# A conv block in five passes: the joins on either side of the second pass, rewritten

## The chip, the cores and the metric

The kernel runs on one core of one Trainium2 chip. The metric is the time of one execution on the device in microseconds (us). Three executions of the kernel before gave 5501.92, 5508.98 and 5525.27; the median, 5508.98, is its time. One further execution was profiled.

## The reference

x has 8 images of 96 x 96 pixels with 192 channels, all in float32. Two residual layers follow each other. What matters here is the first:

```
g      = groupnorm(x)                                  # 32 groups
proj   = g @ W_in + b_in                               # 192 -> 384 channels
local  = depthwise conv 3x3 (proj), zero padding
lr, rl = s[t] = 0.6 s[t-1] + 0.4 local[t], left to right and right to left
tb, bt = the same, downwards and upwards
mixed  = 0.25 (lr + rl + tb + bt) + local
x1     = x + (layernorm(mixed) * ln_g + ln_b) @ W_out + b_out
```

The second layer is: groupnorm of x1, depthwise 7x7 convolution, layernorm over channels, 192 -> 768 -> 192 with a gelu between, scaled and added to x1.

## The kernel before

The program is five passes, with everything between them in DRAM.

**Pass A** (lines 251 to 572) normalises, transposes and projects. It goes over 96 steps: eight images b, four blocks k of eight columns, and three parts j. Each three steps fill one buffer `po` (128 partitions; three blocks m of 128 channels; eight columns), which `store_a` (L425) writes to the DRAM tiles `P_d[g][m]` from the GpSimd (POOL) queue: three large stores `whole` (L430, 1152 KB each) and, where the columns lie at the edge of a 32-column block, small ones `edges` (L442). For the very last `po` the store of m = 0 is split over the POOL and ScalarE (ACT) queues, and the rest is handed on as `late_a`.

**Pass B** (602 to 788) does the convolution and the four scans. It takes 4 channels at a time, k = 0 to 95, in three thirds i: 288 steps n. One step: 24 matmuls on TensorE with a banded matrix (`conv_b`, L662; a float32 matmul shows as two records), copies out of PSUM by ACT (L671, L674), a scan along rows on VectorE (DVE) in one direction (L695) and, one step later, in the other (L704), a small scaling on POOL (L699); the column scans are a matmul (`mix_b`, L683 and L686, copied by ACT in L687), and POOL adds both (L746, three steps after the convolution). The inputs are `pin_k` (partitions 0 to 33 for images 0 to 3, 64 to 97 for images 4 to 7) and `band_k`, loaded from the SyncE (SP) queue by `load_pin_b` (L644, one large and two small DMAs for each half g) and `load_band_b` (L631). They are loaded three k ahead (`load_b(k + 3)`, L758). Each pair of k leaves one buffer `mo`, stored to DRAM by eight DMAs (`store_steps`, L706, issued at L718), two in each step, from the POOL queue; those of the last pair alternate between SP and POOL. `M_d` is two tiles: channels 0 to 255 and channels 256 to 383. Channels are done in order, so the first tile is complete after two thirds of the pass. The last k adds its first third on POOL and the others on DVE (L745).

The start of B, before: L731 to L739 load `pin` for k = 0, 1 with g = 0, then g = 1 and the bands, then everything for k = 2, and then run `late_a`. Images 4 to 7 (g = 1) need the last columns of the last image, so those loads wait for the last stores of A.

**Pass C** (1006 to 1200) turns the image: a unit u is one column of four images, 384 rows by 384 channels, 192 units. `load_c` (L1054) loads `mt` from both parts of M (L1060, 384 KB and 192 KB) and `xr` (L1067). For each of three blocks j, `block_c` (L1073) transposes three channel blocks (L1078), multiplies by the weights `wc` (L1080, three channel blocks accumulated in PSUM), and ACT takes mean and squares (L1082, L1084). POOL adds the constant `cst` to `xr` (L1170), DVE finishes one unit later (L1097). The weights are made at L1018 to L1045: `wc` = W_out scaled by ln_g less its column mean, `cst` = b_out + ln_b W_out; they come from the buffer `pre`, loaded six k before the end of B (L595).

**Passes D and E** (from L852) are the 7x7 convolution and the two dense layers. The change doesn't touch them.

What sets the order: the loops of A to E stand inside `tc.manual_schedule()`, so each engine and queue gets their instructions in the order in which the code calls them. The few statements between the loops (L611 to L613, L1017 to L1045, the three `load_c` at L1139) stand outside, and the planner places them: in the profile L1020 to L1024 run at 756 us, L1018 and the first L1033 at 1789 us. [...] On-chip memory of a finished pass is reused by the next, tile by tile, once the readers of the old tile are done.

## Time and profile before

| | us |
|---|---|
| median of the three timed executions | 5508.98 |
| profiled execution, its own time | 5497.31 |
| its span in the profile | 5495.5 |
| last matmul of A begins | 752.60, runs 2.21 |
| first matmul of B | 772.29 |
| first scan of B on DVE | 778.19 |
| last scans of B on DVE | 1793.25, run 3.37 |
| first transpose of C | 1818.35 |
| third unit of C, its first "mean" on ACT | 1829.23 |
| last matmuls of C, first of D | about 2629 |

In the profiled execution the span is 1.8 us shorter than the device time. A window view lists, for a stretch of the span, the busy time of each engine with the number of instructions, the granted clock of TensorE as a share of full speed (PEclk), the share of time in which the 16 DMA engines were busy, and the GB/s that they moved. A timeline lists instructions in order of their start: start, length, engine, line, operation, tiles, count, and in square brackets how long the engine had been idle and what released it. SPq, ACTq and POOL with DMA_DIRECT2D are the issue of a transfer, not the transfer.

### The profile page before, as it was taken

How to read it: one execution, taken by the hardware profiler on the slowest of the kernel's cores; microseconds unless marked ns; L12 is line 12 of the kernel's file. 1: busy time of each engine (PE TensorE's matmuls, PEld its weight loads, DVE VectorE, ACT ScalarE, POOL GpSimd, SP SyncE). 2: the span in 40 equal slices, each digit the busy share in tenths (PEclk: the TensorE clock that was granted, in tenths of full speed). 3: DMA queues.
4: the chain of work that ended last, by engine and by line, in shares of the span. 5: the costliest groups of instructions: out<-in, count | busy, mean ns of one | idle time of the engine just before them, and what ended most of it. 6: DMA issues, size and time to landing. Idle time of an engine off the chain costs nothing. (4 is left out here: it accounts for less than half of the span.)

```text
span 5495.5 us, 108054 instructions
## 1 busy us (share of the span) xinstructions
PE 5277.4 (96%) x42206; PEld 3357.6 (61%) x42206; DVE 3449.8 (63%) x6722; ACT 2586.1 (47%) x5778; POOL 2367.0 (43%) x2060
## 2 busy tenths in 40 slices
PE   6999989999999899999787899999999999999999
PEld 4666643333333799899444566666666676766767
DVE  6556549999999455555555545555566666656654
ACT  2444447777777466565434444444433333333332
POOL 1211128888888555555322232222233333333332
PEclk9999989999999999999888999999999999999999
DMA  7999869999998799899997454555433232333231
GB/s 219 286 289 276 244 188 245 244 244 243 245 243 218 233 291 294 263 287 308 287 302 176 120 137 121 131 138 136 114 89 80 79 79 79 88 90 86 79 79 41
DMA packets 793246, 1015.28 MB, mean 185 GB/s; under 512 B 331151, under 2 KB 668768, under 8 KB 790688
## 3 DMA queue, kind: packets, MB, share of 16 engines
q1 hardware_dynamic: 676488, 633.41, 44.1%
q0 software_dynamic: 84848, 334.59, 18.5%
q10 hardware_dynamic: 31400, 40.37, 3.3%
q8 instruction: 333, 5.46, 0.4%
q14 instruction: 177, 1.45, 0.1%
HBM read 603.70 MB, written 419.95 MB: 186 GB/s over the span
## 5 line engine op out<-in xcount | busy, mean ns | idle before, releaser
L1481 PEld LDWEIGHTS hp<-w1g,g 128*128 128x128 f32 x6912 | 1117.9, 190 | 140.7 <-issue 83.4
L1481 PE MATMUL hp<-w1g,g 128*128 128x192 f32 x6912 | 1174.9, 329 | 0.0
L1470 ACT ACTIVATE g<-hp,b0g 128x512 f32<-128x512 f32 x864 | 519.8, 692 | 1209.4 <-PE hp L1461 1186.1
L1500 POOL DMA_DIRECT2D out_dram<-xo x288 | 211.3, 734 | 1569.5 <-DVE xo L1492 1488.0
L1492 DVE TENSOR_TENSOR xo<-hp,r 128x384 f32<-128x384 f32 x288 | 229.1, 795 | 983.5 <-PE hp L1481 979.2
L1451 PE MATMUL hp<-yT,w0w 128*128 128x512 f32 x1728 | 779.3, 597 | 19.6 <-DVE yT L1436 19.6
L1080 PE MATMUL po<-wc,mt 128*128 128x193 f32 x3456 | 685.5, 334 | 9.8 <-DVE x1c L1097 9.2
L662 PE MATMUL pl<-pin,band 34*32 34x380 f32 (+1 forms) x13824 | 629.4, 490 | 17.5 <-issue 17.5
L746 POOL TENSOR_TENSOR mo<-mo,z 128x768 f32<-128x768 f32 x286 | 598.9, 2094 | 4.5 <-ACT mo L687 0.4
L1080 PEld LDWEIGHTS po<-wc,mt 128*128 128x128 f32 x3456 | 554.9, 191 | 41.3 <-ACT mean L1082 30.8
L1451 PEld LDWEIGHTS hp<-yT,w0w 128*128 128x128 f32 x1728 | 321.3, 190 | 379.7 <-issue 346.0
L695 DVE TENSOR_TENSOR_SCAN z<-decay,loc 128x768 f32<-128x768 f32 x288 | 505.9, 1757 | 38.7 <-ACT loc L671 9.6
L1244 PE MATMUL hp<-xin,band 63*64 63x372 f32 (+1 forms) x4608 | 420.7, 501 | 95.7 <-ACT yo L1254 35.2
L704 DVE TENSOR_TENSOR_SCAN z<-decay,z 128x768 f32<-128x768 f32 x288 | 498.4, 1731 | 0.1
L662 PEld LDWEIGHTS pl<-pin,band 34*32 34x32 f32 x13824 | 236.1, 107 | 392.8 <-issue 385.9
L1415 POOL TENSOR_TENSOR rs<-tot,neg_half 32x32 f32<-32x32 f32 x72 | 394.7, 5481 | 120.3 <-DVE tot L1413 92.5
L683 PE MATMUL pa<-loc,mix 128*32 128x384 f32 x3456 | 431.9, 493 | 0.0
L686 PE MATMUL pa<-last,down 96*32 96x384 f32 x1152 | 426.8, 493 | 0.9 <-ACT mo L687 0.9
L1461 PE MATMUL hp<-yT,w0w 64*128 64x512 f32 x1728 | 419.5, 611 | 0.0
L1254 ACT ACTIVATE yo<-hp,dwb 128x384 f32<-128x384 f32 x384 | 197.0, 584 | 435.6 <-PE hp L1244 285.0
L671 ACT COPY loc<-pl 128x384 f32<-128x384 f32 x576 | 248.0, 483 | 310.7 <-PE pl L662 310.7
L395 PE MATMUL pm<-xT,win 128*128 128x384 f32 x1152 | 392.4, 491 | 0.0
(155 smaller groups left out, 7237.6 us busy)
## 6 DMA issues: line engine op xcount, KB each, us to landing
pin<-P SPq DMA_DIRECT2D x192, 576.0 KB
P<-po POOLq DMA_DIRECT2D x95, 1152.0 KB, 9.9
mt<-M SPq DMA_DIRECT2D x192, 384.0 KB
xq<-in_x_dram SPq DMA_DIRECT2D x96, 576.0 KB
xr<-in_x_dram SPq DMA_DIRECT2D x192, 288.0 KB
X<-x1c SPq DMA_DIRECT2D x144, 384.0 KB
out_dram<-xo POOLq DMA_DIRECT2D x288, 192.0 KB, 2.5
r<-X SPq DMA_DIRECT2D x35, 1536.0 KB
```

The lines of the kernel that those rows point to most:

```text
L662: nc.tensor.matmul(pls[g][at * RB : (at + 1) * RB, :, lo:hi], band[rows, c, kh, :], pin[rows, c, :, NJ - 1 - j, lo + kh - 1 : hi + kh - 1] ...
L683: nc.tensor.matmul(pa[at], mix[:, i, at], loc[:, q], start=True, stop=True)
L686: nc.tensor.matmul(pa[at], down[:, to], last[:, q], start=True, stop=True)
L695: nc.vector.tensor_tensor_scan(zf, decay_f, loc.rearrange("p q n -> p (q n)"), 0.0, ALU.mult, ALU.add)
L704: nc.vector.tensor_tensor_scan(zr, decay_f, zr, 0.0, ALU.mult, ALU.add)
L746: eng.tensor_tensor(m, m, z, ALU.add)
L1080: nc.tensor.matmul(po, lhs[m], wc[:, m], start=(m == 0), stop=(m == NC - 1))
L1244: nc.tensor.matmul(pys[g][k * 64 : (k + 1) * 64, :, lo:hi], band[rows, k * GS + c, d * ZS : d * ZS + 64], xin[rows, :, :, k * GS + c, lo + ...
L1451: nc.tensor.matmul(hps[m, q], w0w[:, 0, m * 128 : (m + 1) * 128], yT[:, 2 * q], start=True, stop=False,)
L1461: nc.tensor.matmul(hps[m, q], w0w[p, 1, m * 128 : (m + 1) * 128], yT[p, 1], start=False, stop=True,)
L1470: nc.scalar.activation(g[:, m, q], hps[m, q], AF.Gelu, bias=b0g[:, m : m + 1], scale=1.0)
L1481: nc.tensor.matmul(po[:, q], g[:, m, q, k * 128 : (k + 1) * 128], w1g[:, m], start=(m == 0), stop=(m == NE - 1),)
```

## The change

At the join of A and B:

- A DRAM tile `PL_d` holds the last eight columns of the last image for channels 0 to 7 only (73,728 bytes). One DMA on SP writes it from `po`; `last_pin_b` reads it back into `pin_0` (SP) and `pin_1` (ACT), two DMAs each.
- The other parts of `pin_0` and `pin_1` are cut such that they don't touch what the last `po` holds: for g = 1 five DMAs in place of three. They, and the bands, stand ahead of the `PL_d` store on SP.
- The last large stores (`late_a`) are all on POOL now and stand behind steps 1 and 2 of B; `whole(0)` and `edges(0)` are first. The loads of k = 2 follow: half g = 0 in step 0, half g = 1 and the band in step 1, with all of k = 3 behind them.

At the join of B and C:

- The stores of the last `mo` but one go to SP. Those of the last are held back (`late_b`) and issued on ACT in `make_wc`, behind three ACT instructions that scale `wc`.
- All three adds of the last k are on DVE.
- `mean_w` and `lnb` are made on POOL six and four k before the end of B, `wc` is scaled on ACT, `blk` and `pick` are filled on POOL; the matmuls and subtractions of L1036 to L1045 stay, in another order.
- Units 0 to 2 have their `mt` in a tile of the pool `early` (a place that the buffer `yo` of pass D takes later). Their channels 0 to 255 are loaded ahead of the last stores; then, before the rest has come, unit 0 is transposed for those channels and blocks j = 0 and 2 of units 0 and 1 are multiplied for them.
- `block_c` is split into `turn_c`, `project_c` and `square_c`; a third of the channels is left to do for what was begun.
- The two x1c buffers become two pools of one buffer.

And everything from pass A on is put inside one `manual_schedule()`: all in written order.

```diff
+    CC, WA = 4, 8
+    PL_d = dram.tile([WA, 2 * CC, NJ, S], F32, name="PL_d")
...
+            steps = [lambda m=m: whole(m, nc.gpsimd) for m in range(NC)]
+            steps += [lambda m=m: edges(m, nc.gpsimd) for m in range(NC)]
             if final:
-                whole(0, nc.gpsimd, slice(0, 64))
-                edges(0, nc.scalar)
-                whole(0, nc.scalar, slice(64, 128))
-                steps = [lambda m=m: whole(m, nc.gpsimd) for m in range(1, NC)]
-                return steps + [lambda m=m: edges(m, nc.gpsimd) for m in range(1, NC)]
-            for m in range(NC):
-                whole(m, nc.gpsimd)
-            for m in range(NC):
-                edges(m, nc.gpsimd)
+                return steps[::NC] + [f for n, f in enumerate(steps) if n % NC]
+            for step in steps:
+                step()
...
+        ctx.enter_context(tc.manual_schedule())
...
     def load_pre():
+        nc.gpsimd.memset(mean_w, 1.0 / C)
...
+    def spread_pre():
+        for m in range(NC):
+            nc.gpsimd.tensor_copy(lnb[:, m], gb[:, 1, m : m + 1].to_broadcast([128, 128]))
...
+        def load_pin_b(k, g, last=False):
...
+            def part(lo, hi, b=slice(0, GB), j=slice(0, NJ)):
                 nc.sync.dma_start(
-                    pin[p + lo : p + hi].rearrange("p c b j h -> p c (b j h)"),
...
-                )
...
+            if last:
+                part(0, RB - WA)
+                part(RB - WA, RB, slice(0, GB - 1))
+                part(RB, RB + 1, slice(0, GB - 1))
+                part(RB, RB + 1, slice(GB - 1, GB), slice(0, 1))
+            else:
+                part(0, RB)
+                part(RB, RB + 1)
+            part(RB + 1, RB + 2)
+        def last_pin_b(k, eng):
+            pin, p = tiles_b[k], (NG - 1) * 64
+            c = slice(k * CC, (k + 1) * CC)
+            eng.dma_start(
+                pin[p + RB - WA : p + RB, :, GB - 1].rearrange("p c j h -> p c (j h)"),
+                PL_d[:, c].rearrange("r c j h -> r c (j h)"),
+            )
+            eng.dma_start(
+                pin[p + RB : p + RB + 1, :, GB - 1, 1:].rearrange("p c j h -> p c (j h)"),
+                PL_d[WA - 1 :, c, : NJ - 1].rearrange("o c j h -> o c (j h)"),
+            )
...
         with tc.manual_schedule():
             tile_b(2)
             bands_b[0] = tile_band_b(0)
+            for g in range(NG):
+                for k in range(2):
+                    load_pin_b(k, g, g == NG - 1)
             for k in range(2):
-                load_pin_b(k, 0)
-            for k in range(3):
-                for g in range(1 if k < 2 else 0, NG):
-                    load_pin_b(k, g)
                 load_band_b(k)
-            loads = [tiles_b[k] for k in range(3)]
-            for step in late_a:
-                step()
+            nc.sync.dma_start(
+                PL_d.rearrange("r c j h -> c r (j h)"),
+                po[: 2 * CC, 0].rearrange("c r j h -> c r (j h)"),
+            )
+            last_pin_b(0, nc.sync)
+            last_pin_b(1, nc.scalar)
+            loads = [(bands_b[k], tiles_b[k]) for k in range(2)]
             locs, lasts, zs, mos, todo = {}, {}, {}, {}, []
...
-                eng = nc.vector if k == n_k - 1 and i else nc.gpsimd
+                eng = nc.vector if k == n_k - 1 else nc.gpsimd
...
+                if (k, i) == (n_k - 4, 0):
+                    spread_pre()
...
-                        if k + 3 < n_k:
+                        if k == 0:
+                            load_pin_b(2, 0)
+                        elif k + 3 < n_k:
                             loads.append(load_b(k + 3))
...
+                if n == 1:
+                    for step in late_a[:2]:
+                        step()
+                    load_pin_b(2, 1)
+                    load_band_b(2)
+                    loads += [(bands_b[2], tiles_b[2]), load_b(3)]
+                elif n == 2:
+                    for step in late_a[2:]:
+                        step()
...
                     if k == n_k - 1:
-                        for step in todo + store_steps(
-                            mos[k // 2], k // 2, i, (nc.sync, nc.gpsimd)
-                        ):
-                            step()
-                        todo = []
+                        assert not todo
+                        late_b += store_steps(mos[k // 2], k // 2, i, (nc.scalar,))
                     elif k % 2 and i == NI - 1:
                         for i in range(NI):
-                            todo += store_steps(mos[k // 2], k // 2, i)
-            for step in todo:
-                step()
+                            engs = (nc.sync if k == n_k - 3 else nc.gpsimd,)
+                            todo += store_steps(mos[k // 2], k // 2, i, engs)
...
-        nc.vector.tensor_tensor(cst, bo, ps[:, D : 2 * D], ALU.add)
+        def make_wc(stores):
+            ps = ps_s.tile([128, 512], F32, tag="gn_ps", name="ps_w")
+            nc.gpsimd.memset(wc[:, :, D:], 1.0 / C)
+            for m in range(NC):
+                nc.scalar.activation(
+                    wc[:, m, :D], wo[:, m], AF.Identity, scale=gb[:, 0, m : m + 1]
+                )
+            for step in stores:
+                step()
...
+                for m in range(NC):
...
+                    )
+            for m in range(NC):
...
+                nc.gpsimd.tensor_copy(
+                    pick[:, b], ident[:, b * QH : b * QH + 1].to_broadcast([128, 128])
+                )
         M_f = [m.rearrange("w c b h -> w c (b h)") for m in M_d]
         x_f = x.rearrange("b h w c -> (b h) w c")
...
+        first = early.tile([128, NB, NH * NV, GS, WQ], F32, tag="yo", name="mt0")
+        first = first.rearrange("p l n c v -> p (l n c v)")
+        first = first.rearrange("p (u n) -> p u n", n=NC * NH * S)
+        def load_m(u, k):
...
+            if u not in mts and u < 3:
+                mts[u] = first[:, u].rearrange("p (m n) -> p m n", m=NC)
+            elif u not in mts:
+                mts[u] = ip.tile([128, NC, NH * S], F32, tag="mt", name="mt")
+            m = (slice(0, CS // 128), slice(CS // 128, NC))[k]
             nc.sync.dma_start(
-                xr,
+                mts[u][:, m],
+                M_f[k][S - 1 - w, :, hf * NH * S : (hf + 1) * NH * S].rearrange(
+                    "(m c) n -> c m n", c=128
+                ),
+            )
...
         n_u = 2 * PH * WV
-        ahead = [load_c(0), load_c(1), load_c(2)]
         held = x1c = None
         steps, stores, first_d = [], [], []
         with tc.manual_schedule():
+            for u in range(3):
+                load_m(u, 0)
+            make_wc(late_b)
+            for u in range(3):
+                load_m(u, 1)
+            for u in range(3):
+                load_x(u)
+            pos_c = {u: tile_po() for u in range(2)}
+            pts_c = {j: tile_pt() for j in range(NJ3)}
+            for j in range(NJ3):
+                turn_c(mts[0], pts_c[j], j, range(NC - 1))
+            for u in range(2):
+                for j in range(0, NJ3, 2):
+                    project_c(mts[u], pos_c[u][j], j, range(NC - 1))
...
                 if u + 3 < n_u:
-                    ahead.append(load_c(u + 3))
+                    load_c(u + 3)
...
+                    mt, xr = mts.pop(u), xrs.pop(u)
...
+                    ms = [range(NC - 1 if u in pos_c and j != 1 else 0, NC) for j in range(NJ3)]
+                    pos = pos_c.pop(u) if u in pos_c else tile_po()
                     for j in range(NJ3):
-                        block_c(mt, pos[j], var, j)
+                        pt = pts_c.pop(j) if j in pts_c else tile_pt()
+                        turn_c(mt, pt, j, range(0 if u else NC - 1, NC))
+                        project_c(mt, pos[j], j, ms[j])
+                        square_c(pt, pos[j], var, j)
...
-                        x1c = xp.tile([128, NJ3, D, WQ], F32, tag="x1c", name="x1c")
+                        x1c = xps[1 - n % 2].tile([128, NJ3, D, WQ], F32, tag="x1c", name="x1c")
```

## The prediction

> **What bounds the kernel now.** The page's chain of waits names only the dense layers of pass E. That is where the program ends, not where this change acts: a pass that begins earlier shifts all behind it. So I read the chain first, left it, and looked at windows around the two joins, then at their timelines, then at the waits of VectorE inside pass B.
>
> Windows around the first join (columns as explained above; the last two numbers are the DMA share and GB/s):
>
> ```profile
> 740.00:745.00 5.00, 5.00 (x23) 2.88 (x20) 1.82 (x3) 1.97 (x4) 0.00 (x0) 1.00 0.99 376
> 750.00:755.00 5.00, 4.81 (x21) 2.34 (x19) 1.42 (x4) 1.21 (x3) 0.11 (x1) 1.00 0.00 0
> 755.00:760.00 5.00, 0.00 (x0) 0.00 (x0) 1.99 (x10) 0.89 (x2) 3.46 (x5) 0.86 0.78 169
> 765.00:772.00 7.00, 0.00 (x0) 0.00 (x0) 0.00 (x0) 0.00 (x0) 0.00 (x0) 0.50 1.03 368
> 772.00:792.00 20.00, 19.71 (x222) 10.35 (x230) 11.09 (x8) 7.43 (x18) 0.98 (x4) 0.50 0.82 178
> 800.00:1700.00 900.00, 900.00 (x16408) 311.48 (x16400) 872.06 (x514) 637.30 (x1537) 785.31 (x848) 1.00 0.93 243
> ```
>
> Before 755 the DMA engines stand idle while SP waits; from 755 to 772 all engines stand idle while DMA runs full. In steady B, DVE is busy 872 of 900 us: two scans (1.757 and 1.731 us) make the step of 3.5 us. DMA at 0.93 is close behind.
>
> ```profile
> 754.89 2.50 POOL L430 DMA_DIRECT2D P<-po  x3 [18.23 <-ACT po L421]
> ...
> 755.38 0.67 ACTq L430 DMA_DIRECT2D P<-po  x1
> ...
> 760.47 4.26 SPq L644 DMA_DIRECT2D pin<-P  x3
> 764.83 3.26 SPq L631 DMA_DIRECT2D band<-ZB_d  x2
> ...
> 772.29 7.49 PE L662 MATMUL pl<-pin,band 34*32 34x384 f32 x81 [17.48 <-issue]
> ...
> 778.19 1.76 DVE L695 TENSOR_TENSOR_SCAN z<-decay,loc 128x768 f32<-128x768 f32 x1 [3.12 <-ACT loc L671]
> ```
>
> The first join: store issued at 754.9, landed 760.4, a load of 576 KB and the band behind it, TensorE at 772.3. Inside B, DVE waits hardly at all:
>
> ```profile
> DVE z L695 <- ACT loc L671: 9.6, 10, 3.1
> ```
>
> The second join:
>
> ```profile
> 1790.00 1.67 DVE L1033 TENSOR_SCALAR wc<-c_pre 128x192 f32<-128x192 f32 x1
> ...
> 1791.59 1.74 DVE L695 TENSOR_TENSOR_SCAN z<-decay,loc 128x768 f32<-128x768 f32 x1
> ...
> 1793.25 3.37 DVE L704 TENSOR_TENSOR_SCAN z<-decay,z 128x768 f32<-128x768 f32 x2
> ```
> ```profile
> 1802.61 2.01 POOL L746 TENSOR_TENSOR mo<-mo,z 128x768 f32<-128x768 f32 x1
> 1804.64 5.55 SPq L718 DMA_DIRECT2D M<-mo  x5
> ...
> 1815.06 0.89 SPq L1060 DMA_DIRECT2D mt<-M  x2
> ...
> 1818.35 0.96 PE L1078 MATMUL pt<-ident,mt 128*128 128x128 f32 x3 [16.74 <-DMA mt<-M]
> ```
>
> Scans end at 1796.6; the first third's add sits on POOL until 1804.6; the last stores (2304 KB) go then; the load follows at 1815.1. The weight instructions at 1789.4 also push the last scan back.
>
> [...] (0.86 over 755 to 760: down after 3.6 us). [...] the narrow convolution alone ran 16 us at 0.50; full clock came at 792, four us after the matmuls of L683 and L686 began at 788.6. I use the measured ramp. [...] 1815.06 to 1818.35 is 3.29 us for 384 KB, of which 1.07 at 368 GB/s, so 2.2 fixed. [...] L746 on POOL took 3.35 us beside DVE's adds, 2.09 usually.
>
> **Part 1, the small buffer.** Removed from the path: the 5.6 us large store, the 576 KB load, the band behind it. Added: the PL_d store. It needs ACT's copy for m = 0, done at 754.6, so it is issued at 754.8 as POOL's was; 73 KB, 0.2 us of data, 2.2 fixed: 757.2. Then two loads on SP, two on ACT, 0.4 us each to issue, 2.2 to land: 760.1. No row shows a transfer this small; [...] high bound the 5.6 us landing seen under load plus 3.3 (764). I take 760.1: TensorE starts **12.2 us** earlier (8.3 to 12.6). What stands ahead on SP must be gone by 754.8: ten DMAs for g = 1 (0.55 us median each; 1.2 MB, 3.5 us at 370 GB/s) once the k = 2 stores of 734.0 have landed, which the DMA share dates before 745; the four band DMAs (3.3 us at most) need the memory of the last x tile, read until 748.9. That is 752.2: 2.6 us spare in idle DMA time. ACT waits for the PL_d landing with nothing behind it until L671, five us after TensorE's start.
>
> TensorE still idles 5.3 us, beyond 3.6, so starts at half clock as now; the ramp (first mix 16.3 us after the start) is carried over unchanged. No gain, no loss.
>
> **Part 2, the held-back stores.** 3.5 MB of stores plus all of k = 2 move behind B's start. `whole(0)` follows L699 of step 1 on POOL: before, that was 783.92, 11.6 us after TensorE's start, so 771.9. 0.9 to issue, 3.2 of data, 2 to land: 778, `edges(0)` with it. SP then issues pin 2, half g = 1 (576 KB, sharing the engines with the two other stores: 4 to 5 us), and band 2: there by 784.5. Step 6 begins 26.7 us after the start in the profile (798.99 − 772.29), so 786.8: 2.3 us spare, cost 0. If it is late, each us costs one, and beyond 3.6 us of idle the clock falls again: up to 9. K = 3 lies behind it on SP: some 4.3 MB from 776 at 280 GB/s, 791; needed at 797. The debt is paid while no M stores run (the first was at 815, 43 us after the start). On POOL four DMAs in step 2 (2 × 0.89 + 2 × 0.55 = 2.9 us) fit in the 3.8 us step; L699 of step 3 is behind them.
>
> **Part 3, end of B.** Without L1018 and L1033 (0.54 + 1.67) DVE begins the last scan 2.2 us earlier: scans end at 1794.4. Three adds at 1.18: 1798.0. ACT: last copy ends 1795.8, three scalings (not shown; nearest row is L919, 128x192, 0.54 us; between 0.3 and 0.7): 1797.4. Now the stores. Before, 1804.64 to 1815.06, 10.4 us, for the same bytes from two queues; on one queue I take the same, 1807.8. At the 326 GB/s seen best it would be 7.2 + 1.2; if the single queue drains worse, 13. The SP stores, POOL fills and early `mt` loads (1.2 MB, after the last convolution ends at 1788.4: landed by 1795) lie in DMA time that is idle now, and SP idles from 1750 to 1804. They cost nothing; their cover is those idle spans, and an early load that came after 1803 would cost what it is late, up to the 4 us of work done ahead.
>
> **Part 4, C begun.** One 192 KB load: 2.2 + 0.6, TensorE at 1810.6. A hot unit takes 4.13 us: 3 × 0.49 transposes (1.47) and 3 × 0.89 of matmuls net (2.66). Done ahead for unit 0: 2/3 of the transposes and 4/9 of the matmuls, 2.2; it keeps 1.9, at half clock 3.8 less what returns: I take 3.3, end 1813.9. Unit 1 lacks 4/9 of its matmuls, but unit 2 needs PSUM that DVE frees for unit 0: before, unit 0 ended at 1825.1 and its first two L1097 at 1828.0, so 3.0 later: 1816.9. Before, unit 2 began its matmuls with the mean at 1829.23 close to 1829.0. So **12.1 us** earlier (9 to 17 by the store's bounds).
>
> Sum: 12.2 + 12.1 = **24.3**. Against the profiled execution's own time: 5497.3 − 24.3 = 5473.0. The median lies 11.7 above it; the same gain there gives **5484.7**. The other order changes (decay fills, two x1c pools) lie in idle DVE time at 755 to 764.
>
> **The rivals.** (a) Both joins do better: stores at 326 GB/s (2 us), unit 0 hot because the early work keeps the clock up (1.4), wc in time and the PL_d trip at its low bound (0.4), less DMA crowding behind C's start (1 to 3): 30, 5479. For it: the DMA engines are empty at 1795. Against: the last piece waits for the add at 1798. (b) One join is largely lost: pin 2 late by over 3.6 us, the clock falls, 9 lost; 15 left, 5494. For it: margin of 2.3 us. Or the early loads still wait on the last stores, so the change doesn't do what it says there: 12 left, 5497. (c) Slower: the debt isn't paid. DMA at 0.93 has little room; if k = 2 to 5 each come 4 us late, each stop is over 3.6 us, halves the clock and costs 5.5 us more of ramp (step 3, 789.63 to 795.13, took 5.5 in place of 3.5, over some three steps): 4 × 9.5 = 38, less 24.3: 13.7 slower, 5523. It decides from pin 2 landing 31 us after TensorE's start. Against: M stores are absent then.
>
> **Chances.** Forecast (19 to 28 gained) 0.56, (a) 0.21, (b) 0.15, (c) 0.08. 0.5% is 27.5 us, about what a measurement of this kernel can tell from no change. Nearly all of (a), and four tenths of the forecast because the median of three itself moves by several us (5501.9 to 5525.3), read faster: 0.42. Slower beyond it: half of (c), 0.04, and 0.02 for the unseen. Same: 0.52. The range takes in (a) and (b) with the several us by which a median moves: 5479 − 9 = 5470 and 5497 + 5 = 5502. It holds the bounds of every unknown cost above and leaves out (c).
>
> **What would show it.** Right: first L662 within 760 ± 2, first scan near 766, step 6 not waiting on pin or band; the last scan following on the one before it with no L1018 or L1033 between; the first load of channels 256 to 383 some 10 us after ACT's first store; unit 2 of C some 24 us ahead of 1829. Wrong: L662 waiting on P stores; TensorE idle over 3.6 us at step 6; ACT's stores spread over more than 10.4 us.

## The result, and the profile after

The changed kernel takes **5488.14 us** (median of 17 runs, 5481.30 to 5506.06), the kernel before 5505.36 us (17 runs, 5494.27 to 5525.27). The ratio is 0.997, 95% interval 0.996 to 0.998, so some 16.5 us (11 to 22) are gained. The forecast was 5484.7 us in a range of 5470 to 5502, and 24.3 us gained. The profiled execution, however, took 5491.53 us, where the sum said 5473.0. That is 18.5 us off. By the timelines below the first join accounts for 17.5 of them (12.2 forecast, 5.3 lost by step 10); the second gave 1.0 more than forecast, and some 2.0 went elsewhere, which is not explained here.

One mark in the table ahead of the prediction was named wrongly: 1829.23 us is the last "mean" of the **second** unit of pass C (unit 1). Unit 2's transposes begin at 1829.04, which is the value that the working used.

First join, timeline of the changed kernel (start, duration, engine, line, operation, and in brackets the idle time ahead of it with what ended it):

```profile
754.63 0.27 SPq L762 DMA_DIRECT2D PL_d<-po  x1
...
755.50 0.80 PE L688 MATMUL pl<-pin,band 34*32 34x384 f32 x2 [2.13 <-issue]
...
757.20 0.27 SPq L666 DMA_DIRECT2D pin<-PL_d  x1
...
757.84 0.68 ACTq L670 DMA_DIRECT2D pin<-PL_d  x1
...
760.35 8.49 PE L688 MATMUL pl<-pin,band 34*32 34x384 f32 x99 [4.05 <-DMA pin<-PL_d]
...
765.38 1.76 DVE L721 TENSOR_TENSOR_SCAN z<-decay,loc 128x768 f32<-128x768 f32 x1 [10.48 <-ACT loc L697]
```

The short way works: store at 754.63, landed at 757.20, four small loads, TensorE at 760.35 with all but one matmul of the first convolution (one had run at 755.50; the sum said 760.1, the kernel before 772.29), first scan at 765.38 in place of 778.19. So 12.8 us are there at the first scan. Now the windows behind it (the last three numbers are the clock granted to TensorE, the DMA share and GB/s):

```profile
755.00:760.00 5.00, 0.80 (x2) 0.14 (x2) 0.00 (x0) 0.00 (x0) 0.00 (x0) 0.65 0.34 43
775.00:780.00 5.00, 5.00 (x54) 1.26 (x48) 4.59 (x3) 2.51 (x6) 3.98 (x7) 0.50 0.96 345
790.00:795.00 5.00, 5.00 (x56) 1.35 (x56) 3.40 (x2) 2.03 (x5) 2.29 (x2) 0.50 1.00 203
810.00:815.00 5.00, 5.00 (x56) 1.49 (x56) 3.40 (x2) 2.17 (x5) 2.28 (x2) 0.50 0.87 192
820.00:825.00 5.00, 5.00 (x96) 1.63 (x80) 3.92 (x3) 3.43 (x8) 4.25 (x6) 1.00 0.61 167
```

TensorE is busy all the time from 760 on (5.00 of 5.00), but at half clock until 817.9. In the kernel before it was back at 792.7. While it is at half, a step with mix in it (the mix is the matmul of the column scans, from step 3 on) takes 6.71 us in place of 3.51. Where the scan of each step begins, from the two timelines:

| step | 0 | 3 | 4 | 5 | 6 | 7 | 8 | 9 | 10 |
|---|---|---|---|---|---|---|---|---|---|
| before | 778.19 | 789.63 | 795.13 | 798.62 | 802.13 | 805.64 | 809.15 | 812.66 | 816.17 |
| after | 765.38 | 776.82 | 783.55 | 790.26 | 796.98 | 803.69 | 810.40 | 817.12 | 821.51 |
| gained | 12.81 | 12.81 | 11.58 | 8.36 | 5.15 | 1.95 | -1.25 | -4.46 | -5.34 |

Six steps of 6.71 us and one of 4.39 lost 20.1 us; the kernel before lost 2.0 in its step 3. In this execution all of the first join's gain and 5.3 us more were gone by step 10.

Second join, same view:

```profile
1795.17 1.76 DVE L721 TENSOR_TENSOR_SCAN z<-decay,loc 128x768 f32<-128x768 f32 x1
...
1800.14 3.49 DVE L775 TENSOR_TENSOR mo<-mo,z 128x768 f32<-128x768 f32 x3
...
1801.62 0.46 ACT L1065 ACTIVATE wc<-c_pre 128x192 f32<-128x192 f32 x1
1801.78 0.32 ACTq L744 DMA_DIRECT2D M<-mo  x1
...
1803.06 6.12 ACTq L744 DMA_DIRECT2D M<-mo  x6
...
1812.10 1.29 SPq L1111 DMA_DIRECT2D mt<-M  x3
...
1814.48 0.48 PE L1135 MATMUL pt<-ident,mt 128*128 128x128 f32 x1 [7.58 <-DMA mt<-M]
...
1821.96 0.15 ACT L1160 COPY mean<-po 128x1 f32<-128x1 f32 x1
```

The last scan begins 3.51 us after the one before it (1791.66); nothing of pass C stands ahead of it. Scans end at 1800.22. The stores run from 1801.78, the load of the last third goes at 1812.10, 10.3 us later, and TensorE begins on it 14.3 us after the scans' end (before, its first work on any channel began 21.7 us after). The last "mean" of unit 1 comes 21.7 us after the scans' end, before 32.6.

### The profile page after: what moved, and what is told of

The parts are those of the page before. It is cut to its first block, busy times and chain, and to the rows that moved or that the text cites. A ratio compares the mean times of both kernels' runs of the same rounds, so it can differ in the third digit from the quotient of the medians.

```text
span 5489.7 us, 108072 instructions
## 1 busy us (share of the span) xinstructions
PE 5298.0 (97%) x42206; PEld 3359.4 (61%) x42206; DVE 3450.2 (63%) x6706; ACT 2593.6 (47%) x5781; POOL 2366.2 (43%) x2063
## 3 DMA queue, kind: packets, MB, share of 16 engines
q0 software_dynamic: 84304, 331.93, 18.2%
## 5 line engine op out<-in xcount | busy, mean ns | idle before, releaser
L709 PE MATMUL pa<-loc,mix 128*32 128x384 f32 x3456 | 439.4, 500 | 0.0
L712 PE MATMUL pa<-last,down 96*32 96x384 f32 x1152 | 434.2, 500 | 1.0 <-ACT mo L713 1.0
```

Source lines behind the costliest of these rows:

```text
L709: nc.tensor.matmul(pa[at], mix[:, i, at], loc[:, q], start=True, stop=True)
L712: nc.tensor.matmul(pa[at], down[:, to], last[:, q], start=True, stop=True)
```

## The experiments

Theory 1: both joins gain what the sum says, but the clock's return in the first join is not carried over; how late it comes differs from one execution to the next. Theory 2: the return is later by the structure of the changed kernel. Theory 3: the loss is data, the held-back stores and channels 8 to 11. (In the first expectation below, "theory 2" is the prediction as written, the ramp unchanged.) The differences below are against the kernel before on the same chip, from the ratio of the runs, with its 95% interval.

**The first join alone.** The kernel before with the changes to `store_a`, the loads, the prologue of pass B and the held-back stores, nothing of the second join.

> The kernel before with the first join's part of the change alone (small buffer, large stores held back); the second join is as before. Theory 1 (the data path gains 12.8 us, but TensorE's clock comes back later than before and takes back most of it, 0 to 18 us in one execution): first convolution near 760.4, first scan near 765.4, TensorE at 0.50 for 30 us or more from its start in the profiled execution, and 3 to 6 us gained in the median of many. Theory 2 (the prediction as written, the ramp carried over unchanged): 12 us gained, and a clock back some 20 us after the first convolution. Theory 3 (what is lost is waits on data, the held-back stores and k = 2): the clock is back early and VectorE or TensorE wait on pin or band by 5 us or more between 765 and 830.

Measured: 5495.57 us, ratio 0.9983 (0.9968 to 0.9997), 9.4 us gained (2 to 18). The clock was back at 779.8, after 20.5 us at half: theory 1's 30 us or more and its 3 to 6 us did not come, and on the clock this trace fits the ramp as predicted. But this kernel had got a stall of its own, on VectorE's timeline:

```profile
784.15 0.23 DVE L1057 COPY pick<-ident 128x128 f32<-128x128 f32 x1
790.93 0.17 DVE L1060 MEMSET c_pre<- 128x128 f32 x1 [6.54 <-DMA pin<-P]
791.01 1.69 DVE L714 TENSOR_TENSOR_SCAN z<-decay,loc 128x768 f32<-128x768 f32 x1
```

Where the order of pass C's constants isn't written out, one of them landed between two scans of pass B and waited 6.5 us for memory that a load still used, with the next scan behind it in the queue until 791.01; TensorE ran out of work and the clock was at half again from 790.0 to 800.3. In the kernel before the same memset ran at 774.91, where VectorE had nothing to do. So a third kernel:

**The first join alone, in written order.**

```diff
+        ctx.enter_context(tc.manual_schedule())
         with tc.manual_schedule():
             for n in range(NK):
```

> The first join's part alone again, but with the constants of pass C kept in written order behind pass B, as the change has them: in the first such kernel VectorE had a constant of pass C (L1060) in its queue inside pass B, and held step 4 back by some 8 us while that waited for memory. Theory 1: without it 10 to 14 us gained (12.8 of the first join less its ramp, plus 2.2 since nothing of pass C stands ahead of the last scan any more). Rival (the 9 us of the first kernel was the join's own worth): again 9, and steps after 780 no earlier.

Measured: 5491.07 us, ratio 0.9977 (0.9969 to 0.9986), 12.7 us gained (8 to 17); 2.2 of them are the last scan, which belongs to the second join. Its windows show the clock's return:

```profile
785.00:790.00 5.00, 5.00 (x60) 1.24 (x52) 3.12 (x2) 1.50 (x4) 2.27 (x2) 0.50 1.03 283
790.00:795.00 5.00, 5.00 (x76) 1.55 (x72) 3.40 (x2) 2.76 (x7) 1.73 (x2) 0.78 0.94 201
```

792.2 us, with the code of the first join that the changed kernel has. That speaks against a return that is late in every execution.

**The second join alone.** The changed kernel with the first join put back.

> The changed kernel with the first join put back as it was. Theory 1: 13 us gained (2.2 from the last scan, 10.9 from the loads behind the last stores), so that this join gives three quarters of the 17 us measured for both. The prediction as written: 12.1 us. The rival that one join is largely lost, and that it is this one: under 5 us.

Measured: 5490.46 us, ratio 0.9978 (0.9967 to 0.9989), 12.1 us gained (6 to 18). No join is lost, and none carries the whole.

**The changed kernel once more.**

> The changed kernel unaltered, for a second trace of it and as a control. Theory 1 (the ramp's length differs from one execution to the next): 15 to 19 us gained again in the median, but the time at which the clock comes back to 1.00 differs from 817.6 us by over 10 us, and the first ten scans with it. Theory 2 (the ramp is longer by structure in the changed kernel): it comes back within a few us of 817 again.

Measured: 5483.03 us, ratio 0.9962 (0.9947 to 0.9976), 20.9 us gained (13 to 29). The clock came back at 823.5, within 6 us of the first trace and not over 10 us from it. Taken alone that speaks for theory 2; the kernel above with the same first join, at 792.2, speaks against it. Both have a share, as the windows of the clock show below.

```profile
815.00:820.00 5.00, 5.00 (x48) 1.36 (x56) 3.40 (x2) 2.44 (x6) 1.86 (x4) 0.50 0.30 61
820.00:825.00 5.00, 5.00 (x72) 1.38 (x64) 2.36 (x2) 2.66 (x6) 1.93 (x2) 0.65 0.47 135
```

**Idle-time matmuls.** Matmuls of 128x128 by 384 columns whose result nobody reads, ten where TensorE idles in the first join, two in each of the first three steps:

```diff
+            def warm(n):
+                pa = ps_a.tile([128, GB * S], F32, tag="pa", name="pw")
+                for _ in range(n):
+                    nc.tensor.matmul(
+                        pa, ident, mix.rearrange("p j n -> p (j n)"), start=True, stop=True
+                    )
+
+            warm(10)
...
                     locs[k, i] = conv_b(band, pin, i, lasts[k])
+                    if n < 3:
+                        warm(2)
```

> The changed kernel with idle-time matmuls on TensorE that compute nothing used: ten of 128x128 by 384 columns (6.4 us at full clock) behind the end of pass A, and two in each of the first three steps of pass B. Theory 1 (the ramp is the loss): the clock stays at or near 1.00 from 753 us on, steps take 3.5 to 3.8 us from the first, the tenth scan begins near 800 in place of 817, and 8 to 18 us are gained against the changed kernel (25 to 35 against the kernel before). If the data of channels 8 to 11 then come too late, a wait on pin or band of up to 5 us at step 6, near 781, takes part of it back. Theory 3 (data): 0 to 3 us gained over the changed kernel and longer waits on pin. A third: the fillers' own time, about 0.64 us each, delays the first steps by 1 to 4 us and nothing is won.

Measured: 5477.32 us (5474.49 to 5482.04, 6 runs), ratio 0.9949 (0.9933 to 0.9965), 28.1 us gained (19 to 37). The clock stayed at 1.00 until 786. Then, on the timeline:

```profile
782.60 1.76 DVE L721 TENSOR_TENSOR_SCAN z<-decay,loc 128x768 f32<-128x768 f32 x1
...
788.18 4.42 PE L688 MATMUL pl<-pin,band 34*32 34x384 f32 x48 [5.14 <-issue]
...
793.56 1.76 DVE L721 TENSOR_TENSOR_SCAN z<-decay,loc 128x768 f32<-128x768 f32 x1 [7.55 <-ACT loc L697]
```

Step 6 starts 11.0 us after step 5. "issue" means that the profile names nothing that ended the wait; what step 6 needed and had not had before is channels 8 to 11, the last of whose DMAs, for the band, SyncE gave out at 782.04. TensorE waits 5.1 us, the clock falls, the convolution takes 4.42 us in place of 2.15. That the wait is for this data is inferred; two kernels below that send the data sooner lose it. In the changed kernel TensorE did not wait at step 6 (it is busy 5.00 of 5.00 us from 790 to 795, and this convolution begins at 791.92), since the slow clock itself made step 6 late. The ramp and the data cover each other.

**The same in the kernel before**, 26 in its longer gap and two in each of the first three steps.

> The kernel before with the same fillers: 26 in the idle 17.5 us of the first join, two in each of the first three steps of pass B. Theory 1: full clock from the first convolution on, first scan some 2 us after it earlier than before, and 5 to 9 us gained against the kernel before, since it has a ramp too, though in its profiled execution a shorter one. Theory 3: no gain.

Measured: 5496.65 us, ratio 0.9988 (0.9980 to 0.9995), 6.6 us gained (3 to 11). The clock was 1.00 throughout the join, step 10's scan at 811.71 in place of 816.17. So the kernel before pays for this ramp too, and the changed kernel pays more.

**Fillers in the gap only.**

> The changed kernel with the ten idle-time matmuls in the gap only, none in the first three steps. Theory 1, if the idle before the first convolution is what takes the clock down: as good as with the six in the steps, 1.00 throughout from 753. If the narrow convolutions of the first three steps don't keep the clock up by themselves: it falls to 0.50 some 4 to 8 us after the last filler, and the gain over the changed kernel is under 4 us.

Measured: 5477.23 us, ratio 0.9953 (0.9938 to 0.9969), 25.9 us gained (17 to 34). As good as with the six in the steps: the clock stayed at 1.00 until 779.93, through a window that held narrow convolutions alone (762.9 to 766.3). Step 6 came 11.2 us after step 5 (778.05, 789.25), and only there the clock fell.

**Fillers, and the first held-back store sooner.** `late_a[:2]` runs in front of pass B's first step, on GpSimd's queue as before.

> The changed kernel with all fillers (ten in the gap, two in each of the first three steps), and with the first of the held-back stores (m = 0, whole and edges) put on GpSimd's queue before pass B's first step in place of behind step 1. With the fillers alone step 6 waited for channels 8 to 11: its scan began 11.0 us after step 5's in place of 3.5. Theory 1: that wait and the fall of the clock behind it are gone, step 6's scan begins 3.5 us after step 5's, and 7 to 10 us more are gained, near 5468. Rival: the store shares the DMA engines with the small buffer's trip, TensorE starts 1 to 4 us later and the gain shrinks by that. Rival: the wait moves to step 9, for channels 12 to 15, and most of it comes back there.

Measured: 5475.22 us, ratio 0.9946 (0.9932 to 0.9960), 29.7 us gained (22 to 37). The wait at step 6 was gone (785.84, 789.35), but the small buffer paid for it, as one rival said:

```profile
753.61 0.27 SPq L762 DMA_DIRECT2D PL_d<-po  x1
758.53 0.27 SPq L666 DMA_DIRECT2D pin<-PL_d  x1
...
761.71 3.36 PE L688 MATMUL pl<-pin,band 34*32 34x384 f32 x46 [1.48 <-DMA pin<-PL_d]
```

Its trip took 4.9 us beside a store of 1.2 MB, in place of 2.6. Of the 7 to 10 us more that were expected, 1.6 came over the fillers alone, less than the intervals can tell from nothing. The clock fell at 762.5, though TensorE had stood still for 1.5 us only.

**What brings the clock back.** At this point six traces could be laid side by side. From the granted clock in half-microsecond windows, every stretch at half clock in pass B is a multiple of one length: 34.1 us in the kernel before, 61.4 and 68.3 in the two traces of the changed one, 20.5 and 34.1 in the two with the first join alone, 10.2 and 6.8 with fillers. They are 10, 18, 20, 6, 10, 3 and 2 times 3.413 us (61.44 us, 756.46 to 817.90 in the changed kernel, is 18 of them). In each of the 14 traces all stretches at half clock begin on one grid of 3.413 us, and from one trace to the next this grid lies elsewhere against the start of the span (0.28 to 3.32 us). The traces also show what was in a window. I cut each timeline into these windows and added up the mix matmuls (L709, L712, and fillers) in each:

| kernel | windows at half | most mix in one that didn't end it, us | mix in the one that did, us |
|---|---|---|---|
| before | 10 | 0.71 | 2.08 |
| changed | 18 | 1.72 | 1.84 |
| changed, again | 20 | 1.77 | 1.89 |
| first join alone | 6 | 0.00 | 1.80 |
| first join alone, in order | 10 | 1.68 | 1.80 |
| second join alone | 10 | 0.49 | 2.30 |

Whatever the convolutions on 34x32 tiles did (up to all 3.41 us of a window), in these six the clock came back at the end of the first window with 1.80 us of mix or more. A burst of mix is 2.79 us long at half clock. Where a window's edge cut it 1.16 to 1.63, neither part was enough. And a slow step of 6.71 us is nearly two windows (6.83), so the cut moves by 0.11 us a step: in the changed kernel the second part went 1.63, 1.51, 1.41, 1.29 and on down while the first grew from 1.16 over 1.27, 1.38, 1.50, 1.62 and 1.72 to 1.84. This cut lasted six steps.

How the first burst is cut is not pure chance. Pass A too begins slowly: in the changed kernel eight matmuls of 96x96 took 1.52 us at 47.04 and 0.82 at 55.56. The trace's first record of the clock, at 1.00, begins at 53.31 there, which is on the grid, and I take this for the rise; it lies 52 to 56 us into the span, and A's last matmul ends 699.0 to 700.2 us behind this rise in twelve of the 14 traces (702.1 and 702.2 in the two where the clock fell once more in between). So A ends close to an edge, at most 1.1 us before or 0.5 us after it. The first mix follows A's end by 33.8 and 34.0 us with the old first join, which puts it 2.7 and 2.9 us into a window, and both traces took 10 windows. With the new first join and no fillers in the gap (the split kernel below aside) it follows by 22.3 to 22.5 us, which puts it 1.6 to 2.3 us into a window in five of six traces; a burst that begins 1.61 to 2.42 us into one has neither part at 1.80. So the place of the bad cut is the changed kernel's own, as theory 2 has it, and tenths of a us in each execution decide whether it costs 6 windows or 20, as theory 1 has it. How often each comes, one or two traces of a kernel don't tell.

Two kernels were built on this reading of the windows.

**One filler behind each burst** of steps 3 to 11, nothing in the gap:

```diff
                     mix_b(locs.pop((k, i)), lasts[k], mos[k // 2][:, k % 2], i)
+                    if n < 12:
+                        warm(1)
```

> The changed kernel, nothing in the gap, but one idle-time matmul (128x128 by 384, about 1.3 us at half clock) behind the mix matmuls of steps 3 to 11. Theory 1, made exact by six traces: the clock is judged in windows of 3.41 us, and while it is at half it comes back at the end of the first window that holds 1.80 us or more of mix matmuls (L709, L712; all windows with up to 1.77 did not bring it back, whatever the narrow convolutions did). A burst of 2.79 us can be cut in two halves below that, and a cold step of 6.71 us is so close to two windows (6.83) that a bad cut moves by 0.11 us a step and lasts for many steps. With the filler a burst is 4.1 us, which no cut divides into two parts below 1.80: the clock is back within two windows (6.8 us) of the first mix matmul, before 785, in every execution, and 8 to 16 us are gained over the changed kernel less the wait for channels 8 to 11 (up to 8 us). Rival (length of sustained activity, not its share of a window): the return stays as scattered as before, 790 to 823.

Measured: 5490.62 us, ratio 0.9967 (0.9956 to 0.9979), 18.2 us gained (12 to 24), no better than the changed kernel. The clock did what was expected: back at 782.35, in the second window after the first mix matmul (1.66 us in the first, 2.70 in the second), and 9 runs lay within 7.3 us where the changed kernel's 17 spread over 25 and its 8 of the second measurement over 12. (The spread alone proves little: 22 runs of the kernel before with fillers, at full clock in this join, spread over 20.) The time did not, since the filler takes one of the two PSUM tiles (TensorE's output memory) of the mix and waits for ScalarE to empty it, step after step; the waits of TensorE between 783 and 812:

```profile
PE pw L773 <- ACT mo L713: 4.5, 5, 1.0
```

(In total 4.5 us, five times, the longest 1.0.) Steps took 5.1 to 5.4 us at full clock instead of 3.51, through step 12; a filler's own time, 0.67 us by the ten in the gap of the other kernels, is in it too.

**The burst in two halves.** The same matmuls, four of the eight mix groups of a step moved into the middle of its convolution:

```diff
-        def conv_b(band, pin, i, last):
+        def conv_b(band, pin, i, last, half=lambda: None):
...
+                    if (n, at) == (1, 1):
+                        half()
...
-        def mix_b(loc, last, mo, i):
-            for q in range(NG):
+        def mix_b(loc, last, mo, i, qs):
+            for q in qs:
...
+                    half = lambda args=args: mix_b(*args, range(1))
+                    rest = lambda args=args: mix_b(*args, range(1, NG))
```

> The changed kernel, same matmuls, but the mix of a step is done in two halves: the first half (4 of 8 matmul groups) in the middle of the convolution of the step, the second behind it. Theory 1 as made exact: every window of 3.41 us then holds at most some 1.45 us of mix matmuls while the clock is at half, so it never comes back inside pass B: steps stay at 6.7 us in place of 3.51 for some 280 steps, and the kernel is slower by about 900 us, near 6390. Rival (the mean activity decides, or time): the same work per step in another order, so the clock is back between 780 and 825 as before and the time is within 10 us of the changed kernel's.

Measured: **6824.38 us**, ratio 1.2391 (1.2369 to 1.2413), 1316 us slower. The windows of pass B:

```profile
1000.00:1700.00 700.00, 700.00 (x5432) 138.00 (x5416) 288.47 (x170) 219.87 (x509) 257.41 (x283) 0.50 0.43 105
1700.00:3080.00 1380.00, 1380.00 (x10692) 271.99 (x10688) 567.92 (x335) 433.37 (x1002) 510.01 (x560) 0.50 0.42 102
```

TensorE is busy without a break for 2300 us and does not get its full clock: from 757.67 to 3129.93, 695 windows, it stays at half. The first 694 hold at most 1.51 us of mix each. The last, at the end of the pass where little but mix is left, holds 3.33, and with it the clock is back. The size was larger than expected because the split costs work too: a step is 8.27 us (scans at 1003.06 and 1011.33), where 6.7 was expected. As an estimate: half of 8.27 is 4.14, so at full clock the split would cost some 0.6 us a step, 180 us in 288 steps; the other 1,140 would be the clock. The mean share of mix fell with it, 3.0 of 8.27 us in place of 2.8 of 6.7, so a rule on the mean over many windows is not excluded by this kernel alone. It speaks against such a rule that the clock came back in the one window of 3.33, and so do the six traces, where the same work in the same order took between 1 window and 15, from the one in which the first burst began.

**A better version.** The ten fillers in the gap, and the first held-back store on ScalarE's queue, right behind its two loads from the small buffer:

```diff
-            steps = [lambda m=m: whole(m, nc.gpsimd) for m in range(NC)]
-            steps += [lambda m=m: edges(m, nc.gpsimd) for m in range(NC)]
+            engs = [nc.scalar if final and m == 0 else nc.gpsimd for m in range(NC)]
+            steps = [lambda m=m: whole(m, engs[m]) for m in range(NC)]
+            steps += [lambda m=m: edges(m, engs[m]) for m in range(NC)]
...
             last_pin_b(1, nc.scalar)
+            for step in late_a[:2]:
+                step()
```

> The changed kernel with the ten fillers in the gap, and the first of the held-back stores (m = 0) on ScalarE's queue right behind the two loads from the small buffer, so some 8 us earlier than on GpSimd behind step 1, but not beside the small buffer's trip, which a store issued with it had lengthened from 2.6 to 4.9 us. Theory 1: small buffer's trip again 2.6 us, first convolution 6.7 us after pass A's end, clock 1.00 throughout the first join, step 6 without a wait; near 5469, 8 us below the kernel with the fillers alone. Rival: the wait moves to step 9 (channels 12 to 15), and the time stays at 5475 to 5477.

Measured: **5466.25 us** (5457.47 to 5467.27, 5 runs), ratio 0.9920 (0.9905 to 0.9936), 44 us gained (35 to 52). ScalarE's queue, then scans on VectorE:

```profile
759.20 0.68 ACTq L671 DMA_DIRECT2D pin<-PL_d  x1
759.98 0.40 ACTq L430 DMA_DIRECT2D P<-po  x1
```
```profile
783.29 1.74 DVE L722 TENSOR_TENSOR_SCAN z<-decay,loc 128x768 f32<-128x768 f32 x1
784.94 1.74 DVE L731 TENSOR_TENSOR_SCAN z<-decay,z 128x768 f32<-128x768 f32 x1
...
796.62 1.76 DVE L722 TENSOR_TENSOR_SCAN z<-decay,loc 128x768 f32<-128x768 f32 x1
```

The store goes out when the small buffer has landed (2.6 us, as without it). No step waits for data (TensorE stands still once, for 0.4 us), the clock is 1.00 from 753 to 1785, and step 10 is at 796.62, 24.9 us ahead of the changed kernel.

**The store sooner, without fillers.**

> The changed kernel with the first of the held-back stores (m = 0) on ScalarE's queue right behind the loads from the small buffer, as in the best version, but with no idle-time matmuls. It tells how much of the best version's 20 us over the changed kernel is each part's. Theory 1: the two only pay together. While the steps run at half clock step 6 comes late enough by itself (its wait was 1.2 us in the changed kernel), so this alone gives 0 to 4 us over the changed kernel, 5480 to 5488; the clock still falls in the first join and is back between 775 and 825, at the end of the first window of 3.41 us that holds 1.8 us or more of mix matmuls. Rival (channels 8 to 11 are the main loss, the clock a companion of it): 10 us or more over the changed kernel, 5478 or below.

Measured: 5473.76 us (5467.18 to 5485.31, 6 runs), ratio 0.9952 (0.9939 to 0.9965), 26.4 us gained (19 to 34). Theory 1's 0 to 4 us over the changed kernel is missed: it is 5.5 and 9.9 over its two measurements, and the time is below the rival's mark of 5478. But the intervals overlap, and in the profiled execution the clock came back early (779.8, a burst cut 2.50 to 0.21), so how much of it is the store and how much lucky cuts stays open. Step 6 did not wait (783.09, 786.60, 790.11). The 1.2 us that the expectation gives to the changed kernel's step 6 were no wait of TensorE: they are an idle time of its weight loads after 800 us. Over the changed kernel the fillers alone gave 5 to 12 us, the store alone 5.5 to 9.9 and both 23 to 28: more than the sum, though the intervals, some 8 us to either side, don't settle that.

## Why the prediction was right, and where it failed

**Right: the sum of the two joins, with some luck in how near it came.** 5488.14 lies only 3.4 us from the 5484.7 forecast, but the gain missed by 7.8; the rest came off because the kernel before took 5505.36 over 17 runs where the forecast started from 5508.98. In medians the first join gives 12.7 us with the last scan's 2.2 in it, the second 12.1, also with them: 22.6 together against a forecast of 24.3. Measured together they are 16.5 and 20.9, with intervals that reach 22 and 29: the forecast lies above the first and inside the second, so it is a little high, and the ramp below accounts for at least a part.

**Small buffer: mechanism right, size 1.7 us too large.** Counted from the end of pass A on TensorE, which came 1.4 us earlier in the profile after (it lies between 752.1 and 755.7 in the 14 traces), the first convolution (its one early matmul aside) starts 6.98 us later in place of 17.48: 10.5 us gained, and 12.2 were forecast. At the first scan, counted the same way, it is 11.4. The store was to be issued when ScalarE's copy for m = 0 was done (753.17 in the profile after); it went at 754.63, 0.18 after ScalarE's copies for m = 2 had ended (0.18 in the better version too); that it waited for these is likely, not shown. The trip itself was 2.57 us where 2.4 was worked out, and TensorE went on 3.15 us after the first load from the buffer was issued (757.20 to 760.35; 2.9 in the working). The 2.2 us of fixed time in both was the author's estimate from one load of the kernel before, and the 12.6 at the top of the range rested on a shorter trip that no trace shows.

**Failed: "the ramp (first mix 16.3 us after the start) is carried over unchanged. No gain, no loss."** The first mix came 15.4 us after the start, nearly as said. But the ramp did not end some four us after the first mix; in the six traces above it ended with the first window of 3.41 us that held 1.80 us of mix or more. In the kernel before the edge cut the first burst 0.71 to 2.08, so its four us hung on where that burst begins; the change moved the burst, and the edges cut it elsewhere. The four traces with this first join, no filler and the store behind step 1 had the clock back at 779.8, 792.2, 817.9 and 823.5. Against the kernel before, 18.1 us of the profiled execution went this way, from 12.8 gained at the first scan to 5.3 lost at step 10. The median lost a part of that only; with fillers, which take the ramp away, the changed kernel gained 5 to 12 us more (25.9 and 28.1 against 16.5 and 20.9), with intervals that overlap. The reason given for the start at half clock, over 3.6 us of idle time, was read from a single fall (in the kernel before A's last matmul ends at 754.81 and the clock is at half from 758.59). It failed too, though the clock was at half: in the changed kernel TensorE had stood still for 2.1 us and then worked from 755.50 to 756.30, and the clock fell at 756.46, at the end of a window with 1.13 us of work in it.

**The debt of channels 8 to 11: right for the slow clock, wrong for the fast one.** Forecast: there by 784.5, needed at 786.8, cost 0. In the changed kernel the bands went out at 781.8 to 784.4 and TensorE did not wait. But the 26.7 us to step 6 were taken from a profile with a ramp in it. With the clock up, step 6 wants them near 783, and the wait and the fall behind it cost 7.5 us at step 6 and 2.0 at step 7. That is rival (b), "up to 9", which stands ready whenever the ramp is short. In the changed kernel and with fillers alone, late clock or late data kept part of the 12.

**Rival (c) did not come:** no later step waited on pin or band by over 3.6 us in the changed kernel.

**Last stores and pass C: right.** 10.3 us from the first store to the load (10.4 forecast), 10.9 us at unit 1 and 2.2 at the last scan, 13.1 together (12.1). The clock fell for two windows (1811.2 to 1818.0) in place of seven (1799.7 to 1823.6), which the forecast left to rival (a).

**A wrong reading without effect:** steady B was put down to VectorE. In the better version, with work in hand, scans follow each other at 3.29 us a step (783.29 to 786.58) and fall back to 3.51 after step 10, while TensorE's convolutions begin every 3.51 us all along (779.44, 782.95, 786.46). So TensorE makes the step: some 2.15 us of convolution and 1.40 of mix, busy 900 of 900 us.

## What to carry to other kernels

A start-up ramp seen in one profile is no constant: with the same first join it lasted 20.5, 34.1, 61.4 and 68.3 us in four traces, by where the work lay against the clock's windows (3.413 us here). Before carrying it over, cut the timeline into such windows, and look what the first of them hold. Where a change shortens a gap, cost the data behind the gap at the full clock too, for a slow clock hides late data and late data hides a slow clock: step 6 waited for none at half clock here, and with the clock up it lost 7.5 us. Independent matmuls in the gap settle which one it is, and if they sit in PSUM that nobody waits for, they can stay.

## What the runs showed of the hardware

- A TensorE that was busy all the time stayed at half clock for as long as its work was cut the same way: 695 windows, 2372 us, in the split kernel, which was 24% slower. A full window of 34x32 convolutions at half clock (3.41 of 3.41 us) did not end it in any trace; at full clock the clock stayed up through such a window (762.9 to 766.3 with fillers in the gap only).
- The fall came at the edges of the same windows and needed no 3.6 us of idle time: a window that held 0.38 us of fillers and 1.62 of convolutions, with 1.5 us idle, brought it down (762.5), and in the changed kernel one with no idle stretch over 2.2 us and 1.13 us of work (756.46).
- A DMA trip of 73 KB through DRAM took 2.6 us with no large store beside it and 4.9 beside one of 1.2 MB, in one trace.
